# Two double PSUM tiles and four single banks in the first five iterations of the wide attention, three and two from the sixth

## The chip, the cores and the metric

The kernel runs on one core of a Trainium2 chip. The core has a matrix engine (TensorE; "PE" in the profile, with its weight loads shown apart as "PEld"), a vector engine (VectorE, "DVE"), a scalar engine (ScalarE, "ACT"), GpSimd ("POOL") and SyncE ("SP", which here only issues DMAs). TensorE writes its results into PSUM, eight banks of 512 fp32 values in each of 128 partitions; VectorE and ScalarE read them from there. The metric is the device time of one execution in microseconds (us), as the median of several runs.

## The reference

The input x has 8 batches of 512 rows of width 128. The program is two residual layers:

```python
x = x + layernorm(attention(layernorm(x), wq, wk, wv, wo))      # one head of width 128, rope, causal softmax
x = x + layernorm(ffn(layernorm(x), g1, g2, w_down, wq, wk, wv, w_up, router_w, w1, w2, w3))
```

The second layer has inside it an attention of 16 heads of width 4 and a mixture of 8 experts, of which a router picks two for each row. All of it is fp32 to the outside.

## The kernel before

The order of work on every engine is written out by hand: inside `tc.manual_schedule()` each engine issues its instructions in the order in which the program text emits them. What is left to the framework is which buffer of a pool a tile gets, and the semaphores: a tile that takes a buffer waits until every reader of the buffer's last tile is done.

The kernel has three stages. The first is the "wide" attention (the first layer; one head of width 128), batch after batch. The second is the narrow attention of the second layer in 32 "units" (8 batches, 4 groups of heads), which begins inside the end of the first stage. The third is the experts.

**The wide attention.** `wide_attention()` (L1007) is a generator; iteration b works on three batches at once, and yields four times, so the loop that drives it counts i = 4b to 4b+3. For u (batch b), v (batch b-1) and w (batch b-2) the emission order is this:

- i = 4b: `norm` of batch b+1 (four ACT instructions into `xn`), `norm_result` of w (DVE), `project(0)` of u (tile pq), `turn_probs(0, 1)` of v (tile pT_ps), `project(1)` of u (pq);
- i = 4b+1: `turn_probs(2)` and `turn_probs(3)` of v (two tiles pT_ps), `add` of w (DVE, into `x_all`), `values` of u (tile pv), `norm_sum` of w;
- i = 4b+2: `weigh` of v (tile pr, read by DVE into `h_all`), `stats_x` of batch b+2 (DVE), `turn` of batch b+1 (tile xnT_ps), `scores(0)` of u (tile sc);
- i = 4b+3: `scores(1)` of u (sc).

`project` (L258) makes q or k times the two rope tables: four matmuls into pq, one DVE instruction over both banks (`two`), one POOL addition (`roped`). `scores` (L282) makes two row tiles of the scores in one sc tile; for each of them DVE takes the row maximum (`nmax`), then ACT the exponential into `p`, with its row sum read out by a second small ACT instruction, the ACTIVATION_READ_ACCUMULATOR of the profile. The maximum of the second row tile comes after the exponential of the first. `turn_probs` (L308) transposes the exponentials into pT_ps, and ACT copies them to `pT`.

**PSUM.** `banks` (L67) opens pools, `wide(name)` (L74) takes a tile of two banks, `bank(name)` (L77) one of a single bank. Tiles pq, sc and, of the later stages, pqk, sm, sT and ph are wide; pT_ps, pv, pr, xnT_ps, hT_ps, pvs and m3T_ps are single. Until the end of the wide attention there are three wide buffers and two single ones, all eight banks; after it, three wide, one single, and one for po.

**What runs beside it.** After each yield the driving loop (L1065 to L1077) takes steps of other generators: `setup` (weights and tables of the second layer) in iterations 0 to 2; `first` from the fourth, which is `ffn_front(0)` (L521) and then `load_rows(0)` (L574); `fronts` and `units_begin` (the first periods of the units) from iteration 5. `ffn_front` makes hs (POOL), hT (TensorE transposes into hT_ps, copied by ACT), pqk (TensorE, a wide tile, read by DVE), rot and thirds (POOL), and writes these to DRAM on SP's queue; `load_rows` reads them back as q_rows and k_rows. The first tile sm of the units needs these rows.

Of the kernel before, what the change touches and what calls it, by code (L numbers as in the profile page):

```python
# [22 lines left out]
def kernel(  # L23
# [30 lines left out]
    E, _, F = w1.shape  # L54
# [12 lines left out]
    def banks(stack, **bufs):  # L67

        for name, n in bufs.items():
            psum[name] = stack.enter_context(  # L70
                tc.tile_pool(name=f"ps_{name}_{n}", bufs=n, space=bass.MemoryType.PSUM)
            )
# [135 lines left out]
    def fuse_projections():  # L208
        ps = bank("wvo_ps")
        nc.tensor.transpose(ps[:, :P], wv, ident)  # L210
        wvT = work.tile([P, D], F32, tag="sq", name="wvT", bufs=1)
        nc.scalar.copy(wvT, ps[:, :P])
        ps = bank("wvo_ps2")
        nc.tensor.matmul(ps[:, :P], wvT, wo, start=True, stop=True)
        mean = stat.tile([P, 1], F32, tag="wvo_mean", name="wvo_mean", bufs=1)
        nc.vector.tensor_reduce(mean, ps[:, :P], AX.X, ALU.add)
        nc.vector.tensor_scalar(mean, mean, 1.0 / D, None, ALU.mult)
        nc.vector.tensor_scalar(wvo, ps[:, :P], mean, None, ALU.subtract)
# [9 lines left out]
    def stats_x(b):  # L228
        mv, rstd = ln_stats(x_all, b * NT, "x")
        x_stats[b] = minus_product(mv[:, :, 0], rstd, "shift_x", f"shift_x_{b}"), rstd  # L230
# [703 lines left out]
    fronts, backs, later = [], [], []  # L934

    def step(tasks):
        while tasks:
            try:
                next(tasks[0])
                return True  # L940
            except StopIteration:
                tasks.pop(0)
# [11 lines left out]
    def period(n):  # L954
        def of(i):
            return units[i] if 0 <= i < N else None

        before, u, nxt, v = of(n - 1), of(n), of(n + 1), of(n + 2)
        A, C, AC = (0,), (1,), (0, 1)
        if u and u.g == 1 and u.b + 2 < B:  # L960
            fronts.append(ffn_front(u.b + 2))

        def both(t, pairs, unit, parts):
            if v:
                v.rowwise(t, pairs)
            if unit:
                unit.columnwise(parts)
            if v:
                v.highest(t, pairs)
            if unit:  # L970
                unit.weights(parts)

        both(3, A, before, ((2, 0), (2, 1)))
        if before:
            before.weigh(1)
        yield
        both(3, C, None, None)
        if before:
            before.weigh(3)
        if nxt:  # L980
            nxt.turn_m()
        yield
        both(2, A, u, ((0, 0),))
        if before:
            before.weigh(2)
            if before.g == NG - 1:
                backs.append(ffn_back(before.b))
        if u and u.g == 0 and 0 < u.b < B - 1:
            load_rows(u.b + 1)
        yield  # L990
        both(2, C, u, ((0, 1),))
        yield
        both(1, AC, u, ((1, 0), (3, 0)))
        yield
        both(0, AC, u, ((1, 1), (3, 1)))
        if v:
            v.lower()
            v.values()
        yield
        if u:  # L1000
            u.weigh(0)
        yield
# [4 lines left out]
    def wide_attention():  # L1007
        for b in range(B + 1):
            u = batches[b] if b < B else None
            nxt = batches[b + 1] if b + 1 < B else None  # L1010
            v = batches[b - 1] if b > 0 else None
            w = batches[b - 2] if 0 <= b - 2 < CLOSED else None
            if nxt:
                nxt.norm()
            if w:
                w.norm_result()
            if u:
                u.project(0)
            if v:
                v.turn_probs(0, 1)  # L1020
            if u:
                u.project(1)
            yield
            if b == 0:
                fuse_projections()
            if v:
                v.turn_probs(2)
                v.turn_probs(3)
            if w:
                w.add()  # L1030
            if u:
                u.values()
            if w:
                w.norm_sum()
            yield
            if v:
                v.weigh()
            if b + 2 < B:
                stats_x(b + 2)
            if nxt:  # L1040
                nxt.turn()
            if u:
                u.scores(0)
            yield
            if u:
                u.scores(1)
            yield

    def front_and_rows(b):
        yield from ffn_front(b)  # L1050
        yield
        load_rows(b)
# [3 lines left out]
    first = [front_and_rows(0)]  # L1056
    units_begin = [period(-2), period(-1)]
    begun = period(0)
    with tc.manual_schedule():
        banks(ctx, wide=3)  # L1060
        with ExitStack() as stage:
            banks(stage, bank=2)
            batches[0].turn()
            fronts.append(front_and_rows(1))
            for i, _ in enumerate(wide_attention()):  # L1065
                b = i // 4
                if b < 3:
                    step(setup)
                    step(setup)
                elif b < 5:  # L1070
                    step(first)
                    step(first)
                else:
                    step(first)
                    step(fronts)
                    if b > 5 or i % 4 > 1:
                        step(units_begin)  # L1077
            for _ in range(6):
                step(fronts)
                step(units_begin) or next(begun)  # L1080
# [102 lines left out]
```

## Time and profile before

| | |
|---|---|
| median of 3 runs | 792.74 us (791.64 to 792.79) |
| profiled execution: whole time, and span from first to last instruction | 795.85 us, 794.0 us |
| busy over the span: PE, DVE, ACT, POOL | 721.8 us (91%), 489.9 us (62%), 327.9 us (41%), 284.5 us (36%) |
| wide attention's first five iterations, 0 to 82 us; from 24 to 82 us: PE, DVE, ACT, POOL busy | 53.2, 41.0, 28.5, 33.7 of 58 us |
| 82 to 98 us (most of iteration 5): PE, DVE, ACT, POOL busy | 12.6, 10.1, 7.5, 9.2 of 16 us |
| 140 to 440 us (units): PE, DVE, ACT, POOL busy | 268.1, 219.9, 186.3, 184.4 of 300 us |
| 440 to 794 us (experts): PE, DVE busy | 338.0, 182.9 of 354 us |

The span is cut at the first and last instruction; the whole time is 1.85 us longer. Busy times are sums of the durations of instructions on an engine. In a timeline line the columns are the start, the duration, the engine, the source line and operation, the tile written and the tiles read, and how many instructions of the kind are merged; a bracket gives how long the engine had been idle before it and what ended that. In the waits the columns are the engine and line that waited, what it waited for, and the sum, the count and the longest of these waits.

### The profile page before, as it was taken

What the parts mean: (1) busy time and instruction counts of PE and PEld (TensorE: products, weight loads), DVE (VectorE), ACT (ScalarE), POOL (GpSimd) and SP (SyncE); (2) the same over time, 40 slices, a digit from 0 to 9 for tenths busy, and PEclk for the clock granted to TensorE, in tenths of its full rate; (3) what the DMA queues carried; (4) which work ended last, traced back from release to release, by engine and by line L of the source; (5) the groups of instructions that cost most, each with busy time, mean ns of one, the idle gap of its engine ahead of it and who ended that gap; (6) DMA issues with size and microseconds to landing.
All of it is one profiled execution on the core that took longest, in us unless ns stands there. A gap on an engine that the chain in (4) does not pass through costs nothing. (4 is left out here: it accounts for less than half of the span.)

```text
span 794.0 us, 15049 instructions
## 1 busy us (share of the span) xinstructions
PE 721.8 (91%) x5894; PEld 427.5 (54%) x5894; DVE 489.9 (62%) x1090; ACT 327.9 (41%) x515; POOL 284.5 (36%) x596
## 2 busy tenths in 40 slices
PE   4989897888989898998899898999999999999995
PEld 2657565444434444444444465665666666666663
DVE  2486667798867777777773244745554546454544
ACT  2453443575645566666667313222222222222221
POOL 7566542366686867666524030101010101010101
PEclk9999999999999999999999999999999999999998
DMA  9120404040222213223100000000000000000000
GB/s 273 46 81 18 110 11 110 4 109 16 66 58 62 63 49 77 74 51 84 42 3 3 0 1 1 14 0 14 1 14 1 14 2 13 1 14 0 14 1 13
DMA packets 29017, 30.36 MB, mean 38 GB/s; under 512 B 6164, under 2 KB 25332, under 8 KB 28948
## 3 DMA queue, kind: packets, MB, share of 16 engines
q0 software_dynamic: 5280, 14.31, 7.7%
q1 hardware_dynamic: 22516, 14.72, 6.9%
q8 instruction: 46, 0.75, 0.4%
q10 hardware_dynamic: 1152, 0.39, 0.2%
q14 instruction: 23, 0.19, 0.1%
HBM read 15.73 MB, written 11.53 MB: 34 GB/s over the span
## 5 line engine op out<-in xcount | busy, mean ns | idle before, releaser
L633 DVE TENSOR_REDUCE nm<-sm 128x2 f32<-128x1024 f32 (+2 forms) x192 | 194.0, 1042 | 38.0 <-PE sm L601 32.4
L697 ACT ACTIVATE pk<-sT 128x1024 f32<-128x1024 f32 x160 | 161.6, 1024 | 80.0 <-PE sT L601 79.1
L882 ACT ACTIVATE sil<-ph 128x512 f32<-128x512 f32 x128 | 76.4, 597 | 249.9 <-PE ph L874 232.4
L883 DVE TENSOR_TENSOR hid<-sil,ph 128x512 f32<-128x512 f32 x128 | 87.4, 687 | 135.8 <-ACT sil L882 135.8
L895 PEld LDWEIGHTS py<-w2s,hid 128*128 128x128 f32 x1016 | 123.2, 192 | 33.3 <-issue 28.6
L874 PE MATMUL ph<-tT_all,w1s 128*128 128x512 f32 x256 | 131.0, 593 | 0.0
L874 PE MATMUL ph<-tT_all,w3s 128*128 128x512 f32 x256 | 130.7, 592 | 0.0
L895 PE MATMUL py<-w2s,hid 128*128 128x128 f32 x1016 | 124.2, 275 | 3.7 <-DVE o_nat L731 2.0
L169 POOL TENSOR_TENSOR root_o<-ve_o,half 128x4 f32<-128x4 f32 (+1 forms) x9 | 8.6, 959 | 296.2 <-DVE ve_o L186 260.7
L704 PE MATMUL po<-pk,vpad 128*32 128x512 f32 (+3 forms) x1024 | 98.5, 448 | 0.0
L904 DVE SCALAR_TENSOR_TENSOR h_all<-py,gate_all,h_all 128x128 f32<-128x128 f32 x254 | 71.8, 344 | 34.2 <-PE py L895 34.2
L674 PE MATMUL sT<-q_rows,k_rows 64*128 64x384 bf16 (+3 forms) x512 | 64.8, 301 | 18.7 <-DVE nm L633 15.2
L874 PEld LDWEIGHTS ph<-tT_all,w3s 128*128 128x128 f32 x256 | 48.6, 190 | 61.2 <-issue 61.2
L618 PE MATMUL sm<-k_rows,q_rows 61*128 61x256 bf16 (+3 forms) x512 | 71.4, 304 | 5.0 <-ACT pk L697 2.1
L874 PEld LDWEIGHTS ph<-tT_all,w1s 128*128 128x128 f32 x256 | 43.9, 191 | 31.5 <-issue 21.0
L618 PEld LDWEIGHTS <-q_rows 61*128 61x128 bf16 x512 | 23.5, 94 | 56.0 <-issue 51.0
L601 PE MATMUL sm<-ident_bf,mask_q 64*128 64x64 bf16 (+1 forms) x768 | 49.3, 200 | 0.0
L601 PEld LDWEIGHTS <-mask_q 64*128 64x128 bf16 x768 | 38.8, 96 | 12.0 <-issue 0.3
L601 PE MATMUL sT<-ident_bf,mask_k 64*128 64x128 bf16 (+1 forms) x640 | 43.5, 207 | 0.0
L674 PEld LDWEIGHTS <-k_rows 64*128 64x128 bf16 x512 | 26.1, 94 | 31.6 <-issue 30.8
L601 PEld LDWEIGHTS <-mask_k 64*128 64x128 bf16 x640 | 31.2, 95 | 11.5 <-issue 0.5
L452 POOL CAST m<-nm 128x16 bf16<-128x16 f32 x32 | 6.3, 198 | 85.2 <-DVE nm L633 85.1
(178 smaller groups left out, 845.7 us busy)
## 6 DMA issues: line engine op xcount, KB each, us to landing
q_dram<-thirds POOLq DMA_DIRECT2D x18, 192.0 KB, 3.0
k_dram<-thirds POOLq DMA_DIRECT2D x18, 192.0 KB, 3.6
q_rows<-q_dram POOLq DMA_DIRECT2D x12, 288.0 KB, 5.5
k_rows<-k_dram POOLq DMA_DIRECT2D x12, 288.0 KB, 6.9
q_rows<-m3T SPq DMA_DIRECT2D x192, 2.0 KB
x_all<-in_L_attn_x_dram SPq DMA_DIRECT2D x8, 256.0 KB
out_dram<-y SPq DMA_DIRECT2D x7, 256.0 KB
q_dram<-thirds SPq DMA_DIRECT2D x6, 192.0 KB
```

Source lines behind the costliest of these rows:

```text
L169: nc.gpsimd.tensor_tensor(y, x, half[:, :n], ALU.pow)
L601: nc.tensor.matmul(out[:, :, h * HR : (h + 1) * HR], which[at, h, :], ident_bf[at, at].unsqueeze(1).to_broadcast([HR, out.shape[1], HR]), ...
L618: nc.tensor.matmul(sc[:, i, c * n : (c + 1) * n], self.q[at, 2 * self.g + pair, t * P : n], self.k[at, 2 * self.g + pair, :n], start=(c == 0),
L633: nc.vector.tensor_reduce(self.nm[:, :, pairs[0] : pairs[0] + w, t], sc[:, :, : w * n].rearrange("p i (c n) -> p i c n", n=n), AX.X, ALU.m ...
L674: nc.tensor.matmul(sc[:, i, c : c + n], self.k[at, 2 * self.g + pair, j * P : (j + 1) * P], self.q[at, 2 * self.g + pair, j * P :], start= ...
L697: nc.scalar.activation(p[:, :, :c], sc[:, :, :c], AF.Exp, scale=HD**-0.5)
L704: nc.tensor.matmul(po[h * HP : (h + 1) * HP, j * P :], vpads[self.g][:, j, h, :], self.p[j, h // 2][:, h % 2, :], start=(self.g == 0 and j ...
L874: nc.tensor.matmul(ph[:, i, :], w[:, e, c * P : (c + 1) * P], tT_all[:, b, :], start=True, stop=True,)
L882: nc.scalar.activation(sil, ph[:, 0, :], AF.Silu)
L883: nc.vector.tensor_tensor(hid[:, c, :], sil, ph[:, 1, :], ALU.mult)
L895: nc.tensor.matmul(py[:, t * P : (t + 1) * P], hid[:, c, t * P : (t + 1) * P], w2s[:, e, c, :], start=(c == 0), stop=(c == FC - 1),)
L904: nc.vector.scalar_tensor_tensor(h_all[:, n, :], (before if t < NT // 2 else py)[:, t * P : (t + 1) * P], gate_all[:, n, e : e + 1], h_all ...
```

## The change

The order of all instructions stays. Only the pools differ: while i is 0 to 19 (iterations 0 to 4) there are two wide buffers and four single ones. After i = 19 both pools are closed, and pools of three wide and two single buffers are opened, which serve from iteration 5 as the old ones did. The generator is left and taken up again at the same place.

```diff
     with tc.manual_schedule():
-        banks(ctx, wide=3)
+
         with ExitStack() as stage:
-            banks(stage, bank=2)
+            banks(stage, wide=2, bank=4)
             batches[0].turn()
             fronts.append(front_and_rows(1))
-            for i, _ in enumerate(wide_attention()):
+            steps = enumerate(wide_attention())
+            for i, _ in steps:
                 b = i // 4
                 if b < 3:
                     step(setup)
                     step(setup)
-                elif b < 5:
+                else:
                     step(first)
                     step(first)
-                else:
-                    step(first)
-                    step(fronts)
-                    if b > 5 or i % 4 > 1:
-                        step(units_begin)
+                if i == 19:
+                    break
+        banks(ctx, wide=3)
+        with ExitStack() as stage:
+            banks(stage, bank=2)
+            for i, _ in steps:
+                step(first)
+                step(fronts)
+                if i > 21:
+                    step(units_begin)
             for _ in range(6):
                 step(fronts)
                 step(units_begin) or next(begun)
```

## The prediction

> **What bounds the kernel now.** I read the page's busy times first (PE 91% of the span), then the busy times of each stretch, the timeline of the first 100 us, and the waits in front of TensorE from 24 to 92 us. The page's chain of waits gives every step 0% and says nothing here. TensorE is the busiest engine in every stage (53.2 of 58 us in the stretch that the change touches, 268 of 300 in the units, 338 of 354 in the experts), and nothing after the wide attention starts by the clock: a delay of TensorE there moves everything behind it. So I follow TensorE's order and ask what each new assignment of banks makes it wait for.
>
> The waits of TensorE, and of its weight loads, from 24 to 92 us:
>
> ```profile
> PE pT_ps L317 <- ACT pT L320: 3.8, 3, 1.6
> ...
> PE pT_ps L317 <- ACT rope L514: 0.3, 1, 0.3
> ```
>
> ```profile
> PEld pT_ps L317 <- ACT pT L320: 4.9, 4, 1.8
> ```
>
> These are what four single banks remove: with two, the third transposed tile of a batch takes the bank of the first, and waits until ACT has copied it, behind the four `xn` of the next batch. No wide tile waits for its buffer in this stretch; three suffice. Batches 2 and 3, and the start of iteration 5, in the timeline:
>
> ```profile
> 51.09 0.22 PE L292 MATMUL sc<-mask_a,ident_bf 128*128 128x128 bf16 x1
> 51.09 0.30 PEld L262 LDWEIGHTS pq<-xnT,wqk 128*128 128x128 f32 x2 [0.33 <-issue]
> 51.14 1.51 PE L262 MATMUL pq<-xnT,wqk 128*128 128x512 f32 x3
> ...
> 52.61 0.19 ACT L299 ACTIVATION_READ_ACCUMULATOR p<-sc,nmax 128x1 f32 x1
> ```
>
> ```profile
> 81.83 1.94 PE L262 MATMUL pq<-xnT,wqk 128*128 128x512 f32 x4
> ...
> 84.75 0.44 PE L317 MATMUL pT_ps<-ident,p 128*128 128x128 f32 x2 [0.72 <-ACT p L299]
> 85.02 1.88 PE L262 MATMUL pq<-xnT,wqk 128*128 128x512 f32 x4
> ...
> 86.67 0.19 ACT L299 ACTIVATION_READ_ACCUMULATOR p<-sc,nmax 128x1 f32 x1
> ...
> 88.81 0.65 PE L317 MATMUL pT_ps<-ident,p 128*128 128x128 f32 x4 [1.58 <-ACT pT L320]
> ...
> 95.30 0.37 PE L618 MATMUL sm<-k_rows,q_rows 61*128 61x512 bf16 x1 [1.08 <-DMA k_rows<-k_dram]
> ```
>
> The reader is to see that pq follows the last score matmul at once, while ACT's exponentials of those scores end later: the second at 52.80 (52.61 + 0.19), and for batch 4 the fourth at 86.86. The third wide buffer is what lets TensorE run ahead of them.
>
> **The change, part by part.** The bank tiles come in the order pT, pT, pT, pv, pr, xnT; the wide ones pq, pq, sc, sc. With two wide buffers, the first pq of a batch takes the buffer of the last batch's first sc, and waits for its second exponential; the second pq takes the other sc's, and waits for the fourth. After an exponential's read-out TensorE starts 0.05 to 0.1 us later (84.69 to 84.75). All shifts below are against the old times; a plus is later.
>
> *Batch 1* (27.8 us on): the second exponential ended at 26.7, so pq waits for nothing. The 0.30 us for the rope copy goes, and some 0.1 before pv: **-0.35**.
>
> *Batch 2*: TensorE would be free at 39.0. The second exponential ends at 40.37, now 40.02: pq starts at 40.07 instead of 39.40 (+0.67). The second pq (41.50 + 0.67) just meets the fourth exponential (42.53 - 0.35). The third transposed tile's wait of 0.78 us goes; it runs at 44.4 instead of 44.49: **-0.1**. DVE's `two` of the second pq ends 0.1 later (45.42 for 45.32), and with it DVE's dense chain of adds, moments and maxima behind it.
>
> *Batch 3*: the second exponential now ends at 52.9, so pq starts at 52.95 instead of 51.14: 1.8 us, of which TensorE stands idle 1.75. The wait of 1.48 us before the third transposed tile goes; pv is **+0.45**. The second `two` (DVE), then `roped` and hs (POOL) are +0.6, and with them the transposes of hT, for which TensorE already waited: +0.6 until sc. Then pqk takes a wide buffer too, so the second sc takes that of the first and waits for its second exponential: read out at 69.7 where TensorE is free at 68.9, 0.85 us more: **+1.5**.
>
> *Batch 4*: pq meets its exponentials; 0.3 us of weight loads goes, none of TensorE's. TensorE stays +1.5, DVE is +1.7 (second `two` at 76.5 for 74.76).
>
> *The new pools at i = 20*: no new instruction. But the new wide pool lies on banks of both old pools. The framework states for its pools, by default, that every tile of such a pool waits for every user of the pools below; the trace has no such switch that costs a visible wait. Bounds: if only the banks' own last tile counts and that is the first sc, pq waits for the second exponential, 84.69 + 1.7 = 86.4; if all users count (or the bank's last tile is the second sc, which the rotation gives: pqk shifted it into the first buffer), for the fourth, 86.86 + 1.7 = 88.56. I take the latter. pq starts at 88.6 for 81.83, **+6.8**, with TensorE idle from 83.45: 5.1 us. Queued behind that pq on TensorE is everything.
>
> What is late next: the old run waited here too. Of the +6.8, 0.72 and some 0.2 (transposes for the first exponentials), 1.58 (ACT's copy, since `xn` now runs before pq) and 1.08 (rows by DMA) were waits that the later start covers; together 3.6 to 3.8. DVE's and POOL's work for the rows is +1.7, so these land at about 97.0, before sm comes at 98.3. At the second sc of batch 5 TensorE is at 98.65 for 95.66: **+3.0**. From there the buffers are the old ones, and the shift stays.
>
> *The clock.* Where TensorE did little from 58.5 to 61.3 us (one pv's end and four spread transposes), its granted clock fell:
>
> ```profile
> 61.00:62.00 1.00, 0.90 (x7) 0.89 (x7) 0.30 (x3) 0.52 (x1) 0.76 (x2) 0.76 0.06 23
> 62.00:63.00 1.00, 1.00 (x7) 1.00 (x7) 0.00 (x0) 0.07 (x1) 0.95 (x1) 0.50 0.07 16
> 63.00:64.00 1.00, 1.00 (x6) 1.00 (x6) 0.00 (x0) 0.00 (x0) 0.60 (x3) 0.50 0.00 0
> 64.00:65.00 1.00, 1.00 (x7) 1.00 (x6) 0.00 (x0) 0.00 (x0) 0.00 (x0) 0.53 0.00 0
> ```
>
> Behind the stretch and its length come the busy times of PE, PEld, DVE, ACT and POOL, and then the clock: 0.50. The 20 matmuls of pr took 4.02 us there, 2.44 elsewhere: 1.6 lost. The Trainium skill, "TensorE: Matmul & The Clock Gate", Part 1, says that one idle window of some 3.4 us halves the clock, in windows that run free of the kernel. By the rule, 5.1 us of idleness hold a whole window in (5.1 - 3.4)/3.4, half of the cases, at 1.7 us (3.4 us at half speed): 0.85 on average (an estimate from that page). By the row, 2.8 us of thin work are enough, and the cost is 1.6. I take the row: +1.6, with 0 and 3.4 as ends. The same page's section on a second failure mode (cycling through few PSUM banks makes TensorE idle shortly, and the clock swings) speaks against two wide buffers as such: the gaps of 1.05, 1.75 and 0.85 us would each cost up to 1.7, some 5 us in all. The row speaks against that: idle stretches of 0.72 and 1.58 us from 82 to 90 us left the clock at 1.00. I take nothing for these gaps.
>
> **Sum**: 3.0 + 1.6 = +4.6 us on the profiled execution's 795.85. The same stages run in the unprofiled runs, whose median of 792.74 is 0.4% less; the shift is carried over as it is: **797.3 us**.
>
> **The rivals.**
>
> 1. *The freed banks win* (faster). The removed waits (0.3, 0.78, 1.48, 0.3) are 2.9 us: 789.8 if the new waits of pq cost nothing. That would be so if the maxima of the scores began earlier when pr runs earlier, by more than pq waits; it decides where the row maximum waits for pr's reader on DVE. For it: at 36.62 DVE did wait 2.98 us for pr. Against it: in batches 2 and 4 DVE came to `h_all` after pr had ended (49.01 after 48.32, 80.90 after 79.0), so there DVE's own chain sets the exponentials.
>
> 2. *The switch costs nothing, or little.* With pq at 86.4 or before, the rows from DRAM, +1.7 through DVE and POOL, still hold sm, which in the old run waited for exactly these: +1.7, **794.5**. For it: only two sc tiles are in flight. Against it: both of them end under the banks of the new pool.
>
> 3. *All as forecast, but the clock holds*: +3.0, **795.7**. For it: the windows run free, and the idle stretch may not fill one.
>
> 4. *No effect*: the waits exchange evenly and TensorE's slack in iteration 5 takes up the rest: 792.7. Against it is the 1.08 us wait for the rows, which is no slack once the rows are late too.
>
> **How the numbers follow.** A measurement of this kernel tells 0.2% (1.6 us) from no change. Chances: the forecast with the clock's fall (795.8 to 799.6) 0.51; rival 3 0.17; rival 2 0.12, half of it within 0.2%; rival 1 0.10; rival 4 0.05; still more (a second fall of the clock, or a switch that drains more than I count) 0.05. So slower 0.51 + 0.17 + 0.06 + 0.05 = 0.79, same 0.06 + 0.05 = 0.11, faster 0.10. The range leaves out rival 1, rival 4 and the last: 793.2 to 799.6.
>
> **What would show it.** Right: no wait of pT_ps for ACT's pT before iteration 5; from batch 2 on, pq waits for ACT's `p` by 1 to 1.8 us; the second sc of batch 3 waits 0.85 us for `p`; TensorE stands 4 to 6 us before iteration 5's first pq, with the clock near 0.5 behind it; sm no longer waits for k_rows; the old and new timelines stay 3 to 5 us apart from 100 us on. Wrong: pq at i = 20 that starts within 2 us of the scores before it (then rival 2), or a first sm earlier than 93.8 (rival 1), or a gap that closes again in the units, which would mean that TensorE's order is not what sets their end.

## The result

The changed kernel takes 799.56 us (median of 7 runs, 797.8 to 806.34), the kernel before 793.34 us (median of 7 runs beside it): a ratio of 1.007, 95% interval 1.0042 to 1.0098. It is slower by 0.4 to 1.0%. The profiled execution has a span of 798.1 us (before: 794.0).

The two profiles differ in their first 24 us, for the most part by chance: TensorE's clock came up earlier in the profile of after (its first eight pq matmuls took 5.36 us, before 6.62), and in the profile of before it fell once more (to 0.64 from 20 to 22 us and 0.51 from 22 to 24 us, where after had 1.00). So I compare from batch 1's first pq (27.84 us before, 24.80 after, 3.04 us apart), and mean by **stretch A** the time from there to batch 5's second sc (95.66 and 97.12 us), by **stretch B** the time from there to the first po of the units (140.1 and 144.4 us). A went from 67.8 to 72.3 us, B from 112.3 to 119.6. Behind the first po the two profiles take the same time: 653.9 and 653.7 us. All that is lost between these two profiles is lost before it.

TensorE's waits in the profile of after, 24 to 92 us (who waited for what: sum, times, longest):

```profile
PE pq L262 <- ACT p L299: 8.0, 3, 5.3
PE hT_ps L199 <- POOL hs L463: 1.6, 1, 1.6
PE sc L291 <- ACT p L299: 0.8, 1, 0.8
PE rope_ps L199 <- DVE rope_wide L505: 0.3, 1, 0.3
```

The 3.8 us of waits for ACT's pT are gone. In their place stand 8.0 us in which pq waits for the exponentials, in three places: 0.86 us in batch 2, 1.81 in batch 3, and 5.31 at the switch of the pools. Batch 3 and the switch in the timeline of after:

```profile
47.28 0.22 PE L292 MATMUL sc<-mask_a,ident_bf 128*128 128x128 bf16 x1
...
49.05 0.19 ACT L299 ACTIVATION_READ_ACCUMULATOR p<-sc,nmax 128x1 f32 x1
...
49.30 1.98 PE L262 MATMUL pq<-xnT,wqk 128*128 128x512 f32 x4 [1.81 <-ACT p L299]
```

```profile
79.61 0.22 PE L292 MATMUL sc<-mask_a,ident_bf 128*128 128x128 bf16 x1
...
82.73 0.19 ACT L299 ACTIVATION_READ_ACCUMULATOR p<-sc,nmax 128x1 f32 x1
...
84.89 0.19 ACT L299 ACTIVATION_READ_ACCUMULATOR p<-sc,nmax 128x1 f32 x1
...
85.14 3.78 PE L262 MATMUL pq<-xnT,wqk 128*128 128x512 f32 x4 [5.31 <-ACT p L299]
```

Before, pq started 0.05 us after the start of the scores' last matmul in both places. Now it stands behind the second exponential's read-out in batch 3, which ends at 49.24 (49.05 + 0.19), and at the switch behind the fourth, which ends at 85.08, not the second (82.92). Those four matmuls took 3.78 us instead of 1.94. The reason is in the stretches of after (length, busy PE, PEld, DVE, ACT, POOL, then the clock):

```profile
82.00:84.00 2.00, 0.00 (x0) 0.00 (x0) 1.20 (x3) 1.19 (x4) 0.87 (x3) 0.64 0.35 115
84.00:86.00 2.00, 0.86 (x1) 0.50 (x2) 0.27 (x1) 1.69 (x5) 0.00 (x0) 0.50 0.58 154
86.00:88.00 2.00, 2.00 (x4) 0.81 (x3) 0.00 (x0) 0.62 (x2) 0.00 (x0) 0.50 0.79 181
88.00:90.00 2.00, 2.00 (x7) 1.14 (x6) 0.97 (x1) 0.36 (x1) 0.00 (x0) 0.65 0.83 185
```

The clock is 0.50 while it is down, so 0.64 in the first row means that it fell at about 82.6 us, 2.7 us after the last score matmul ended (79.83), and 0.65 in the last row that it came back at about 89.4. It was down for 6.8 us, and TensorE worked in the last 4.3 of them.

The first sm of the units no longer waits for its rows:

```profile
96.74 0.39 PE L618 MATMUL sm<-k_rows,q_rows 61*128 61x512 bf16 x2
```

### The profile page after: what moved, and what is told of

Its sections match the earlier page's. It is cut to its first block, busy times and chain, and to the rows that moved or that the text cites. A ratio compares the mean times of both kernels' runs of the same rounds, so it can differ in the third digit from the quotient of the medians.

```text
span 798.1 us, 15055 instructions
## 1 busy us (share of the span) xinstructions
PE 722.1 (90%) x5894; PEld 428.3 (54%) x5894; DVE 489.7 (61%) x1090; ACT 328.0 (41%) x515; POOL 285.0 (36%) x596
## 5 line engine op out<-in xcount | busy, mean ns | idle before, releaser
L262 PE MATMUL pq<-xnT,wqk 128*128 128x512 f32 x64 | 34.6, 670 | 9.8 <-ACT p L299 8.4
```

The lines of the kernel that those rows point to most:

```text
L262: nc.tensor.matmul(pq[:, s, :], wqk[:, i, s, :], self.xnT, start=True, stop=True)
```

## The experiments

All times are medians of five rounds or more, with the ratio to the kernel before on the same chip. A and B are of the profiled execution; the mean clock is that of all its runs. The kernel before was measured again beside each group of kernels: its line is the one beside e1 to e4 with eight; beside the changed kernel it took 793.34 us, beside e4 with five to e7 794.25 (mean clock 0.9891), beside e8 and e9 794.45 (0.9887).

| kernel | time, us | ratio (95%) | A, us | B, us | mean clock |
|---|---|---|---|---|---|
| before | 793.95 (19 runs) | | 67.8 | 112.3 | 0.9887 |
| changed | 799.56 | 1.007 (1.0042 to 1.0098) | 72.3 | 119.6 | 0.9843 |
| e1, switch alone | 798.86 | 1.0063 (1.004 to 1.0085) | 69.7 | 117.0 | 0.9850 |
| e2, two and two | 802.61 | 1.0103 (1.0075 to 1.0132) | 73.1 | 120.4 | 0.9820 |
| e3, switch after i = 17 | 794.18 | 1.0003 (0.9987 to 1.002) | 68.1 | 113.3 | 0.9898 |
| e4, eight matmuls in the gap | 799.03 | 1.0066 (1.0043 to 1.009) | 71.7 | 117.4 | 0.9891 |
| e4, five matmuls | 798.45 | 1.0083 (1.0058 to 1.0108) | 70.3 | 116.0 | 0.9870 |
| e5, waits by tile | 797.1 | 1.0038 (1.0017 to 1.0059) | 68.1 | 113.9 | 0.9881 |
| e6, xn later | 795.86 | 1.003 (1.0012 to 1.0048) | 66.4 | 111.1 | 0.9849 |
| e7, xn and hT later | 796.95 | 1.0048 (1.0023 to 1.0074) | 67.3 | 113.4 | 0.9857 |
| e8, xn later, hT before the scores | 790.31 | 0.9951 (0.993 to 0.9972) | 63.7 | 108.5 | 0.9901 |
| e9, hT before the scores | 793.06 | 0.9985 (0.9964 to 1.0006) | 64.7 | 111.0 | 0.9886 |

**e1: the switch alone.** The pools keep their sizes, but are closed and opened again.

```diff
-            banks(stage, wide=2, bank=4)
+            banks(stage, wide=3, bank=2)
```

> Three wide and two single buffers all through, as before, but both pools are closed and opened again after i = 19. Theory (a tile of the new pools waits for every user of the old ones): iteration 5's first pq starts about 5 us later than the scores before it end, after the fourth exponential of batch 4 (before: 81.83 us, now about 86.9), TensorE's clock falls to 0.5 behind the gap (about 2 us lost), the wait of sm for the rows goes, and the kernel is 3 to 4 us slower than before. Rival (the switch costs nothing, the two wide buffers cost it all): no gap, within 1 us of before.

The timeline of e1:

```profile
78.34 0.22 PE L292 MATMUL sc<-mask_a,ident_bf 128*128 128x128 bf16 x1
83.47 3.78 PE L262 MATMUL pq<-xnT,wqk 128*128 128x512 f32 x4 [4.92 <-ACT p L299]
```

The gap is there (4.92 us) with nothing changed but the boundary of the pools, and so are the four slow matmuls. Stretch A is 1.85 us longer than before, in a profile in which the clock did not fall near 60 us (pr took 2.40 there, before 4.02); with that fall it would be some 3.5 us. The time rose by 4.9 us, of the 6.2 that the whole change costs, and by more than the 3 to 4 that I expected. The rival falls.

**e2: two wide, two single.**

```diff
-            banks(stage, wide=2, bank=4)
+            banks(stage, wide=2, bank=2)
```

> The changed kernel with two single buffers instead of four in the first five iterations (two banks unused). Theory A (in the changed kernel the four single banks give back what the profile of before shows as waits for ACT's pT, 0.8 to 1.5 us in each of batches 2 and 3): 2 to 3 us slower than the changed kernel, with waits of pT_ps for ACT's pT of this size. Theory B (with two wide buffers the second pq waits for the fourth exponential, so ACT has long copied the first pT when the third comes): within 0.7 us of the changed kernel and no such waits over 0.3 us.

TensorE's waits in e2, 24 to 96 us:

```profile
PE pq L262 <- ACT p L299: 7.2, 3, 4.9
PE hT_ps L199 <- POOL hs L463: 1.2, 1, 1.2
PE sc L291 <- ACT p L299: 0.8, 1, 0.8
PE rope_ps L199 <- DVE rope_wide L505: 0.4, 1, 0.4
PE pT_ps L317 <- ACT rope L514: 0.3, 1, 0.3
```

No wait for ACT's pT, with only two single banks. So the four banks were not needed to remove them: the second pq now starts when the fourth exponential is done, and while TensorE works at it, ACT gets through `xn` and the copy of the first pT. What two more banks give is 0.8 us in stretch A (the wait for the rope copy, and 0.3 us before each pv). The time lies 3 us from the changed kernel's, further than theory B has it and as far as theory A has it (1.0103 against 1.007, intervals overlapping), with a lower mean clock. The waits decide for B; the time alone would not, and why the clock was lower is not shown.

**e3: the switch two steps earlier.** The order of the instructions stays.

```diff
-                if i == 19:
+                if i == 17:
                     break
...
                 step(first)
-                step(fronts)
+                step(first if i < 20 else fronts)
```

> The changed kernel with the switch of the pools two steps earlier, after i = 17, before batch 4's scores; the order of all instructions stays. Theory (the place of the switch is what costs): the new pools' first tile is pr, which waits for ACT's last copies only (under 1 us), batch 5's pq has the third wide buffer, the gap of 5.3 us and the fall of the clock behind it go: 3 to 5 us faster than the changed kernel, 0 to 2 us slower than before. Rival (two wide buffers cost it, wherever the switch is): within 1.5 us of the changed kernel.

```profile
75.08 2.50 PE L327 MATMUL pr<-v,pT 128*128 128x128 f32 x20 [0.68 <-ACT v L280]
...
80.34 0.22 PE L292 MATMUL sc<-mask_a,ident_bf 128*128 128x128 bf16 x1
80.40 1.94 PE L262 MATMUL pq<-xnT,wqk 128*128 128x512 f32 x4
```

The boundary of the pools now costs 0.68 us before pr, and pq follows the scores at once. The kernel is level with before (1.0003). The three waits that two wide buffers bring are all there (0.86 and 1.81 us before pq, 0.81 us before the second sc of batch 3), and still, with two wide buffers kept for all but the last scores, the change costs nothing that can be measured: its price is where the pools are switched.

**e4: TensorE kept busy in the gap.** Eight, then five matmuls whose result is not used.

```diff
                 if i == 19:
+                    warm = bank("warm")
+                    for _ in range(8):
+                        nc.tensor.matmul(
+                            warm, wqk[:, 0, 0, :], batches[5].xnT, start=True, stop=True
+                        )
                     break
```

> The changed kernel with eight matmuls of 128x512 (their result is not used) on TensorE behind batch 4's scores, in the gap before iteration 5's first pq; some 4 us of work in 5.3 us of waiting. Theory (the clock's fall behind the gap costs 2 us of the change): no stretch of 0.5 there, the first pq's four matmuls take 2.0 instead of 3.8 us, 1.5 to 2 us faster than the changed kernel. Rival (the slow clock is hidden beside other waits): within 0.5 us of it.

Eight took 7.09 us, more than the gap: each of them is two matmuls in the trace (16 in all). The clock held, but pq came 1.8 us later behind the scores; A is still 0.6 us shorter than the changed kernel's. The time is level with it (1.0066 against 1.007), where I expected 1.5 to 2 us less.

> The changed kernel with five matmuls of 128x512 whose result is not used behind batch 4's scores; in the run with eight they took 7.1 us, more than the gap of 5.3 us, so that the first pq came 1.8 us late and nothing could be read from the time. Five are 4.4 us. Theory (the clock's fall behind the gap costs 2 us): no stretch of 0.5 there, pq starts at the same distance behind the scores as in the changed kernel, its four matmuls take 2.0 instead of 3.8 us, and from batch 1's first pq to batch 5's second sc it is 2.0 us shorter than the changed kernel's 72.3. Rival (the slow clock is hidden beside other waits): within 0.5 us of 72.3.

The same with five; the first pq in the timeline, and the stretches around it:

```profile
85.27 1.98 PE L262 MATMUL pq<-xnT,wqk 128*128 128x512 f32 x4 [0.98 <-ACT p L299]
```

```profile
82.00:84.00 2.00, 2.00 (x6) 0.74 (x4) 1.18 (x3) 1.20 (x4) 0.99 (x3) 1.00 0.39 129
84.00:86.00 2.00, 1.01 (x3) 0.49 (x3) 0.40 (x1) 1.56 (x5) 0.00 (x0) 1.00 0.48 153
86.00:88.00 2.00, 2.00 (x8) 1.00 (x7) 0.64 (x1) 1.09 (x3) 0.00 (x0) 1.00 0.80 204
```

The clock stays at 1.00, and A is 70.28 us for 72.32: the fall of the clock behind the gap costs 2.04 us there, as expected. In the time of the whole kernel this can't be seen (1.0083 against 1.007, intervals overlapping). Why is not shown; single runs of one kernel differ by more than these 2 us, and their mean clocks with them.

**e5: pools that wait by tile.** The pools' option `reuse_waits="tile"` makes a tile wait for the last users of its own banks alone, and the single banks are placed first, so that the new wide tiles land on them. Its lines lie five further down (L267 is L262).

```diff
-            banks(stage, wide=2, bank=4)
+            banks(stage, bank=4, wide=2)
...
-                tc.tile_pool(name=f"ps_{name}_{n}", bufs=n, space=bass.MemoryType.PSUM)
+                tc.tile_pool(name=f"ps_{name}_{n}", bufs=n, space=bass.MemoryType.PSUM, reuse_waits="tile")
```

> The changed kernel with pools whose tiles wait only for the last users of their own banks, and with the four single banks placed below the two wide ones, so that iteration 5's first pq lands on banks of long finished single tiles. Theory (the gap is the wait of the new pools for batch 4's fourth exponential, not the order of the work): no gap before pq, no fall of the clock, 3 to 5 us faster than the changed kernel and within 2 us of before; what stays is the lateness of the rows. Rival (some other user of the banks, or the boundary of the pools itself, holds TensorE): the gap stays, within 1 us of the changed kernel.

```profile
78.94 1.94 PE L267 MATMUL pq<-xnT,wqk 128*128 128x512 f32 x4
82.27 0.55 PE L322 MATMUL pT_ps<-ident,p 128*128 128x128 f32 x3 [1.39 <-ACT p L304]
84.43 3.52 PE L267 MATMUL pq<-xnT,wqk 128*128 128x512 f32 x4 [1.62 <-ACT p L304]
```

The first pq starts at once; what is left are the transposes' own wait for the exponentials (1.39) and one of the second pq (1.62). That the clock would not fall was wrong: TensorE was busy for only 0.55 us from 82 to 84 us, and from 84 to 86 us the clock was 0.54 (the four matmuls of the second pq took 3.52 us). A is 68.1, 0.3 us more than before, in a profile in which the clock did not fall near 60 us (pr took 2.40 there). The theory holds for the gap. The time is 2.9 us above before, more than the 2 us I allowed.

**e6: the waits for pT removed in another way.** Pools as before; only the place of `xn` in ACT's order.

```diff
-            if nxt:
-                nxt.norm()
             if w:
                 w.norm_result()
...
                 v.turn_probs(2)
                 v.turn_probs(3)
+            if nxt:
+                nxt.norm()
```

> The kernel before with the four xn instructions of the next batch emitted behind the third transposed tile instead of at the start of the iteration (pools as before, three and two). Theory (the waits of pT_ps that four single banks were to remove come from ACT's order, not from a lack of banks): no wait of pT_ps for ACT's pT over 0.4 us from batch 2 on, 1 to 3 us faster than before. Rival (ACT only moves the wait to xnT_ps or pr): those wait as long, within 1 us of before.

TensorE's waits, 24 to 96 us:

```profile
PE hT_ps L199 <- POOL hs L463: 2.7, 1, 2.7
PE pT_ps L317 <- ACT p L299: 1.1, 2, 0.7
PE sm L618 <- DMA k_rows<-k_dram: 0.8, 1, 0.8
...
```

The waits for pT are gone without one more bank, and A is 1.4 us shorter than before. But TensorE then waits 2.7 instead of 1.3 us for hs, and the kernel is slower (1.003). B is 1.1 us shorter in the profile, but the profiled execution is the fastest of the 12, and their mean clock is 0.9849 against 0.9891 of the kernel before beside them. The expectation of the time was wrong; what lowered the clock is not shown.

**e7: hT behind the scores of batch 3.**

```diff
                 elif b < 5:
                     step(first)
-                    step(first)
+                    if i != 13:
+                        step(first)
```

> As e6_norm_later, and hT of the second layer's first batch is emitted one step later, behind pr and the first scores of batch 3, so that TensorE does not wait for hs with pr behind it. Theory (that wait of 1.3 us and the 1.6 us of slow clock behind it are on the path): no stretch of 0.5 near 60 us, 2 to 4 us faster than before, at the cost of at most 0.5 us where the rows come later. Rival (the rows from DRAM then hold sm): within 1 us of e6_norm_later.

```profile
65.57 1.99 PE L535 MATMUL pqk<-hT,wqk 128*128 128x512 f32 x4 [2.60 <-ACT hT L530]
```

The clock held near 60 us, as expected (pr took 2.40 us). But the wait only changed its place: ACT copies hT behind the exponentials, and pqk waits 2.6 us for it. The kernel is slower than before (1.0048). The theory falls.

**e8 and e9: hT between xnT_ps and the scores.** In e8 on top of e6, in e9 alone.

```diff
                 nxt.turn()
+            if b == 3:
+                step(first)
             if u:
                 u.scores(0)
...
                     step(first)
-                    step(first)
+                    if i != 13:
+                        step(first)
```

> e6_norm_later, with hT of the second layer's first batch emitted behind pr and xnT_ps of batch 3 and ahead of its scores (in e7 it stood behind the scores, so that ACT copied it behind their exponentials, and pqk waited 2.6 us). Theory (the path from 24 to 96 us is TensorE's, and hs is what it waits for): the wait for hs falls from 2.7 to under 2 us, no slow clock near 60 us; from batch 1's first pq to batch 5's second sc 63 to 65.5 us (before 67.8, e6 66.4); the kernel 1 to 3 us faster than before. Rival (the rows from DRAM hold sm, or the clock falls later and takes it back): stretch or time within 1 us of before.

The timeline of e8:

```profile
57.48 0.60 PE L199 MATMUL xnT_ps<-ident,xn 128*128 128x128 f32 x4
58.85 0.96 PE L199 MATMUL hT_ps<-ident,hs 128*128 128x128 f32 x4 [0.77 <-ACT xnT L256]
...
60.48 1.98 PE L535 MATMUL pqk<-hT,wqk 128*128 128x512 f32 x4
```

hs is all but done by then (it ends at 59.42); hT waits 0.77 us for ACT's copy of xnT, pqk for nothing, and the clock holds near 60 us (pr took 2.40 us, before 4.02). A is 63.7 us, 4.1 less than before, of which the clock makes 1.6. The kernel takes 790.31 us, 0.9951 of before (0.993 to 0.9972): it is faster than before, by 4.1 us where I expected 1 to 3.

> The kernel before with the move of hT of e8 alone (pools and xn as before). Theory: as e8, without the 1.4 us that the later xn gave in e6: stretch 65 to 66.5 us, the kernel 0.5 to 2.5 us faster than before. Rival: as in e8, within 1 us of before.

A is 64.7, shorter than expected, but B is only 1.2 us under before (in its profile the clock falls twice between 124 and 140 us, to 0.50), and the time (0.9985, 0.9964 to 1.0006) can't be told from it.

## Why the prediction was right, and where it was not

The sign and the main mechanism were right, and the time (799.56 for 797.3) lies in the range, 0.04 us under its end of 799.6. That is in part luck: the range had room for a dearer fall of the clock at the switch, while what was missing in the forecast lay elsewhere (below). By the prediction's own steps, after taking off the 3.04 us between the two profiles' beginnings:

| step | predicted | measured |
|---|---|---|
| batch 1, at pr | -0.35 us | -0.91 |
| batch 2, first pq: idle before it; shift | 1.05; +0.67 | 0.86; +0.11 |
| batch 3, first pq: idle before it; shift | 1.75; +1.8 | 1.81; +1.20 |
| batch 3, second sc: wait; shift | 0.85; +1.5 | 0.81; +0.95 |
| first pq behind the switch: idle before it; shift | 5.1; +6.8 | 5.31; +6.35 |
| fall of the clock behind it | 1.6 | 2.04 (e4 with five) |
| batch 5, second sc: shift with the clock | +4.6 | +4.50 |
| first po: shift | +4.6 | +7.3 |

**The waits of pq** were right in each place, to about 0.2 us. The shifts are all some 0.5 to 0.6 us too high from batch 1 on, because the gain there was mis-sized: the wait for the rope copy made 0.5 us on TensorE, and I counted 0.30; and before pv the weight loads had waited for ACT's copy of pT, which made 0.4 us, and I counted 0.1. In the waits of before:

```profile
PEld pv L272 <- ACT pT L320: 0.4, 1, 0.4
```

**That it takes four banks to remove the waits for pT** was the step whose reason failed. The waits went, but e2 has none of them with two banks: they belonged to a second pq that ran ahead of the exponentials, and the two wide buffers ended that. The sum was not hurt, as I had counted the waits as gone; but a design that spends two more banks on it buys little (0.8 us of A in e2). e6 shows the other cause: where ACT copies pT ahead of `xn`, two banks do.

**The switch** was the unknown between "second exponential" and "fourth"; I took the fourth, and after shows it (85.14 behind 85.08). e1 shows the gap with the old sizes, e3 and e5 show it gone when the pools change at another place or wait by tile. **The rows from DRAM** ceased to be waited for, as predicted; that 1.08 us with the waits of 0.72 and 1.58 makes 3.4 of the 3.9 us by which 6.35 shrank to 2.46 without the clock (4.50 - 2.04).

**The clock at the switch.** The prediction set a rule (one whole idle window of 3.4 us) against a row of the trace of before (2.8 us of thin work), and took the row. It held: the clock fell 2.7 us after the last score matmul had ended, before 3.4 idle us had passed. Its price was too low: the clock was down for 6.8 us, not 3.4, and at half speed the 4.3 us of work in them lose about 2.1, where 2.04 was measured. So the +4.50 beside the forecast's +4.6 is luck in its parts: 2.46 for 3.0 without the clock, 2.04 for 1.6 with it. The other idle gaps (0.86, 1.81 and 0.81 us) brought no fall, as assumed; the section that the prediction cites for them speaks of cycling through banks in each iteration, not of few banks.

**What the prediction missed** lies behind 96 us. It said that "the shift stays" from there; but it grew from 4.50 to 7.3 us, in three places. Both pq of batch 6 wait in the profile of after, for the maxima of sm and for an exponential, and did not before; this makes 1.2 us:

```profile
100.53 1.98 PE L262 MATMUL pq<-xnT,wqk 128*128 128x512 f32 x4 [0.64 <-DVE nm L633]
...
103.22 1.99 PE L262 MATMUL pq<-xnT,wqk 128*128 128x512 f32 x4 [0.39 <-ACT p L299]
```

The second of them before:

```profile
100.55 1.98 PE L262 MATMUL pq<-xnT,wqk 128*128 128x512 f32 x4
```

And the clock falls once more, at a pr of after that took 2.50 us before; this makes 1.6:

```profile
132.82 0.65 PE L317 MATMUL pT_ps<-ident,p 128*128 128x128 f32 x4 [1.36 <-ACT pT L320]
...
133.86 4.07 PE L327 MATMUL pr<-v,pT 128*128 128x128 f32 x20
```

```profile
131.17 2.50 PE L327 MATMUL pr<-v,pT 128*128 128x128 f32 x20
```

The 1.2 us stand in e1, e2, both e4 and e5 as well, in e5 although its second sc is only 0.3 us late; so they come from neither the gap nor the clock alone. What makes these maxima and exponentials late was not followed. The fall at this pr is in e1, e2 and e9 too, and not in e3, both e4 and e5. The wait of 1.36 us in front of it is the same before and after. Whether the fall follows from the gap at the switch or from where the windows happened to lie is open. The mean clock does not settle it: 0.9843 against 0.9887 (of the kernel before beside e1) is 0.0044 less, and the fall of 6.8 us at the switch alone makes 0.5 x 6.8 / 794 = 0.0043.

Of the rivals, "the freed banks win" and "no effect" fail on the time, which is clear of before, "the switch costs little" on the gap of 5.31 us and on e1, "the clock holds" on the rows of after. Of the prediction's own signs one failed: the timelines did not stay 3 to 5 us apart from 100 us on.

## What to carry to other kernels

A change of PSUM pools in mid-stream is a wait like any other: with these pools' default, the first tile behind it waits for the last reader of all the tiles below. Put it where those have long been read (here before the scores: 0.68 us), not where the longest chain of readers is just beginning (5.3 us). And before giving a bank to a wait for a copy, look at what stands ahead of that copy on its engine.

## What the runs showed of the hardware

Single runs of the kernel before differ by 6 us (791.32 to 797.66 in 19 runs), and the mean clock goes with it: 0.992 to 0.993 in the four fastest (791.3 to 791.6 us), 0.984 in the two slowest of 796.9 and 797.7. So a shortened stretch need not show in the time: e6 saved 1.4 us in A, and its 12 runs were slower all the same, with a mean clock of 0.9849.

The record of the clock in the traces has falls of 3.41 us and of 6.83 us: of 6.83 behind each gap of about 5 us (changed kernel, e1, e2), and now and then in the units and the experts (e2, e7, e8). A gap of 1.8 us in front of pq never brought one. In front of batch 3's pr, TensorE has some 3 us of thin work, from the end of pv on: a wait for hs and four transposes. It brought a fall in before (2.8 us), in the changed kernel (3.1), in e2, e3, both e4 and, with 4.2 us, in e6. It brought none in e1 (2.8 us) and e5 (3.1). So the same work may or may not bring a fall.
